# A four-layer graph kernel: late slabs, their sign tests and two weight loads moved within layer 0

## The chip, the cores and the metric

The kernel runs on one core of one Trainium2 chip. The metric is the device time of one execution in microseconds.

## The reference, cut to what matters

x is 2708 x 512, adj is 2708 x 2708, non-negative, with a full diagonal and few other entries. Four layers follow one another, each with a layer norm in front and a residual:

```
h = relu(layernorm(x));  x = x + layer0(h, adj)   # (adj + head) @ h / row sum; head = (adj > 0) / sqrt(count of adj > 0)
h = relu(layernorm(x));  x = x + attention(h, adj)        # scores - 1e16 * (1 - adj), softmax, 8 heads
h = relu(layernorm(x));  x = x + tanh(relu(adj @ (relu(adj @ (h @ W1) + b1) @ W3) + b3) @ Wf + bf)
h = relu(layernorm(x));  x = x + (adj != 0) @ (h @ W + b) / column count
```

With the factor 1e16 the softmax of attention picks one entry of each row, so the kernel only looks for the largest entry of each row of adj (a "search" of the row) and gathers one projected row. It sets flags ("bad") where an input doesn't allow such shortcuts: a negative entry of adj, a tie, weights so large that scores could reach the mask. A general path, in a branch at the end, is taken only then.

## The kernel before

Rows are cut into 22 row tiles of 128 (the last has 20 rows). Layer 0 and the projections of attention are done in one loop over m = 0 to 21, and this loop fills the first third of the time. In turn m:

- PE adds up the products of row tile m into acc (L778), from the incidence blocks that DVE made one turn ahead (`incidence(m + 1)`, lines L617 to L649). These need the norm of the row, spread over the partitions by a product into the PSUM tile rb (L619). The pool of rb has one buffer, and `score_bound` takes the same one for its sum (L466).
- DVE then finishes the row tile: xt (L787), and the statistics of its norm (L172 to L179). ACT applies the norm (hn, L182), PE transposes it (pt, L188), ACT copies it (hT, L189), PE projects it (yacc, L158): that is `after(m - 1)`.
- `stats_to` works ahead on the slabs, the 128 rows of adj that belong to a row tile (1.35 MB, tile name ar, three buffers): signs and counts on ACT (L510, L515), row sums (L529), and the search for the largest entry on DVE (`attended`, L540 to L549: MAX8 and FIND_INDEX8, about 3 us each). The three ar buffers serve the rank lists too (`rank_rows`, `load_ranks` of the last row tile).
- POOL gathers rows of h and blocks of adj by lists (L562, L580), which DVE has made by `search` (L372 to L400) from the ranks.

Row tiles 3, 4, 5, 0, 1, 2 (LATE, in this order) come first in the statistics, and their slabs are dropped there without a search. They are read again in turns m = 15 to 20, one to a turn, for the test for negative entries (`count_signs`: Sign at L497, Relu at L498, compared at L489) and the search. In before, turn 15 asks for the slabs of 3 and 4, and each later turn for the next one.

`score_bound` reads Wq and Wk (1 MB each), squares and sums them on ACT (L464), and makes one flag. `load_w` and `split_w` read W1 (then W3) into one buffer (wr) and split W1 on ACT and DVE (L193 to L203). `behind(dst, last)` is a DVE copy of one element from `last` into `dst` (L425): what writes `dst` afterwards has to wait for it.

A planner of the framework sets the order of the instructions on each engine before the run, the program's order being the priority; it may put a later instruction of the program ahead of an earlier one that isn't ready by its own reckoning. Each engine then works its queue in that order.

Of the kernel before, what the change touches and what calls it, by code (L numbers as in the profile page):

```python
# [42 lines left out]
def kernel(  # L43
# [31 lines left out]
    NT = (N + P - 1) // P  # L75
# [11 lines left out]
    def rows(t):  # L87
        return min(P, N - t * P)

    def dense_of(m):  # L90

        return 0 if m == NT - 1 else DENSE
# [127 lines left out]
    with tc.tile_pool(name="l0_slab", bufs=2) as slabs, tc.tile_pool(  # L220
# [202 lines left out]
        def behind(dst, last):  # L423

            nc.vector.tensor_copy(dst, last)  # L425
# [51 lines left out]
        LATE = FIRST + ZERO  # L477
        masks, row, slab = {}, {}, {}

        def load_slab(m):  # L480
            n = rows(m)
            if m in slab:
                return
            slab[m] = slabs.tile([P, N], FP, name="ar", bufs=3)
            nc.sync.dma_start(out=slab[m][:n], in_=adj[m * P : m * P + n])

        def flag_negative(m, sum_sgn, cnt):
            n = rows(m)
            nc.vector.tensor_tensor(  # L489
                bad[:n, BAD_NEG + m : BAD_NEG + m + 1], sum_sgn[:n], cnt[:n], ALU.not_equal  # L490
            )

        def count_signs(m):

            sgn = slabs.tile([P, N], BF, name="sgn", bufs=GROUP)
            cnt, sum_sgn = (wp.tile([P, 1], FP, name=name, bufs=4) for name in ("cnt", "sum_sgn"))
            nc.scalar.activation(sgn, slab[m], AF.Sign, accum_out=sum_sgn)  # L497
            nc.scalar.activation(sgn, sgn, AF.Relu, accum_out=cnt)  # L498
            flag_negative(m, sum_sgn, cnt)

        def row_norm(m):


            n = rows(m)
            ar = slab[m]

            cnt, sum_sgn = (wp.tile([P, 1], FP, name=name, bufs=4) for name in ("cnt", "sum_sgn"))
            rn, deg = (wp.tile([P, 1], FP, name=name, bufs=10) for name in ("rn", "deg"))
            sgn = slabs.tile([P, N], BF, name="sgn", bufs=GROUP)
            nc.scalar.activation(sgn[:n], ar[:n], AF.Sign, accum_out=sum_sgn[:n])  # L510
            if m in LATE:
                cnt = sum_sgn
                nc.vector.tensor_scalar_max(cnt[:n], cnt[:n], 0.0)
            else:
                nc.scalar.activation(sgn[:n], sgn[:n], AF.Relu, accum_out=cnt[:n])  # L515
            nc.scalar.activation(rn[:n], cnt[:n], AF.Sqrt)
            nc.vector.tensor_scalar_max(rn[:n], rn[:n], NORM_EPS)
            nc.vector.reciprocal(rn[:n], rn[:n])
            if m not in LATE:
                flag_negative(m, sum_sgn, cnt)  # L520
            masks[m], row[m] = sgn, (rn, deg, cnt)
# [13 lines left out]
        def attended(m):  # L535

            n = rows(m)
            cols = slice(m * P, m * P + n)
            ar = slab.pop(m)
            nc.vector.tensor_max(ar[:n, cols], ar[:n, cols], ident[:n, :n])  # L540
            top = wp.tile([P, 8], FP, name="top")
            nc.vector.max(top[:n], ar[:n])
            at_top = wp.tile([P, 8], U32, name="at_top")
            nc.vector.max_index(at_top[:n], top[:n], ar[:n])
            nc.vector.tensor_copy(idx[:n, m : m + 1], at_top[:n, 0:1])
            nc.vector.tensor_scalar(
                top[:n, 0:2], top[:n, 0:2], 1.0, MASK_SCALE, op0=ALU.subtract, op1=ALU.mult
            )
            nc.vector.tensor_tensor(  # L549
                bad[:n, m : m + 1], top[:n, 1:2], top[:n, 0:1], ALU.is_ge  # L550
            )
# [104 lines left out]


        order_n = ZERO[:1] + FIRST + ZERO[1:] + list(range(LEAD + GROUP, NT))
        late = list(LATE)
        normed, near, far = [0], [LEAD], [LEAD]  # L660
        listable = set()

# [3 lines left out]
        def do_next(num=1):  # L666
            for job in todo[:num]:
                if job.func is search and job.args[0] not in ranks_of:
                    load_ranks(job.args[0])
                job()  # L670
                if job.func is search:
                    listable.add(job.args[0])
            del todo[:num]
            if todo and todo[0].func is search and todo[0].args[0] not in ranks_of:
                load_ranks(todo[0].args[0])

        def stats_to(m):


            while normed[0] <= order_n.index(m):  # L680
                t = order_n[normed[0]]
                do_next()
                load_slab(t)
                if normed[0] + 1 < NT:
                    load_slab(order_n[normed[0] + 1])
                row_norm(t)
                row_sum(t)
                if t == 0 or t % GROUP == GROUP - 1 or t >= NT - 2:
                    last_block = count(masks)
                    if t not in ZERO:  # L690
                        if dense_of(t):
                            rank_blocks(list(masks), last_block)
                        else:
                            flush_counts()
                            todo.append(partial(rank_rows, list(masks)))
                        todo.extend(partial(search, k) for k in masks)
                        do_next(0)
                    masks.clear()
                if t in late:
                    slab.pop(t)  # L700
                else:
                    attended(t)
                normed[0] += 1
# [32 lines left out]
        def flush_counts():  # L736
            for issue in pending_c:
                issue()
            pending_c.clear()
# [26 lines left out]
        for m in range(NT):  # L766
            n = rows(m)
            if m + 1 < NT:
                load_x(m + 1)
            if m + 2 < NT and m + 2 >= LEAD and dense_of(m + 2):  # L770
                blocks[m + 2] = load_block(m + 2, tiles_d)
            flush()
            if LEAD <= m + 1 < NT:
                incs[m + 1] = incidence(m + 1)
            acc = ps_acc.tile([P, D], FP, name="acc")
            pairs = incs.pop(m)
            for i, (a, g) in enumerate(pairs):
                nc.tensor.matmul(  # L778
                    acc[:n], a, g, start=(i == 0), stop=(i == len(pairs) - 1)
                )  # L780
            if m + 1 < LEAD:
                stats_to(m + 1)
                incs[m + 1] = incidence(m + 1)
            if m:
                after(m - 1, hns.pop(m - 1))
            xt = xs.pop(m)
            nc.vector.scalar_tensor_tensor(  # L787
                xt[:n], acc[:n], row.pop(m)[1][:n], xt[:n], op0=ALU.mult, op1=ALU.add
            )
            hns[m] = wp.tile([P, D], FP, name="hn")  # L790
            norm(wp, xt, n, hns[m])
            store(m, xt)
            if normed[0] == NT:
                do_next(2 if NT - 8 < m < NT - 5 else 1)
            stats_to(min(2 * m + 6, m + 8, NT - 1))
            gathers_to(m + 2)
            if m + 8 > NT and late:
                if late[0] not in slab:
                    load_slab(late[0])
                if len(late) > 1:  # L800
                    load_slab(late[1])
                count_signs(late[0])
                attended(late.pop(0))
            if m + 8 == NT + 1:
                todo.append(partial(rank_rows, list(range(1, LEAD))))
                todo.extend(partial(search, k) for k in range(1, LEAD))
            if m == NT // 2 + 4:
                score_bound(xt[:1, :1])
            if m == NT - LEAD - 1:
                for t in range(1, LEAD):  # L810
                    gather_adj(t)
            if m == NT // 2 + 6:
                wr = load_w(wset, w1_d, "wr", lambda w: behind(w[:1, 0, :1], xt[:1, :1]))
                w1 = split_w(wset, wr, "wa")
                wr = load_w(wset, w3_d, "wr")
# [430 lines left out]
    for m in order_2:  # L1246
# [16 lines left out]
        if m == NFULL:  # L1263
            xt = wp.tile([P, D], FP, name="u")
        else:

            place = {order_2[-1]: "gs0", NSLOT: f"slot{order_2[-1]}"}.get(m, f"slot{m}")
            xt = x3[m] = gp.tile([P, D], FP, name=place)
# [55 lines left out]
    with tc.If(general > 0):  # L1324

        with tc.tile_pool(name="l0_g", bufs=2) as gp, tc.tile_pool(
# [3 lines left out]
            for t in range(NT):  # L1330
                n = rows(t)
                xt = gp.tile([P, D], FP, name="xt")
# [4 lines left out]
            for m in range(NT):  # L1337
# [35 lines left out]
                xt = gp.tile([P, D], FP, name="xt")  # L1373
# [7 lines left out]
        with tc.tile_pool(name="l1_qkv", bufs=1) as qkvp:  # L1381
# [6 lines left out]
            with tc.tile_pool(name="l1_pw", bufs=1) as pwp, tc.tile_pool(  # L1388
# [13 lines left out]
                for b in range(NB):  # L1402
# [4 lines left out]
                    for t in tiles:  # L1407
                        n = rows(t)
                        o = t * P - c0
                        xt = pxp.tile([P, D], FP, name="xt")  # L1410
# [116 lines left out]
        with ExitStack() as gen:  # L1527
# [94 lines left out]
            for t in range(NT):  # L1622
                n = rows(t)
                xt = wp.tile([P, D], FP, name="xt")
# [19 lines left out]
            for block in range(NB):  # L1644
# [4 lines left out]
                for t in node_tiles(c0, nb):  # L1649
                    n = rows(t)  # L1650
                    xt = wp.tile([P, D], FP, name="xt")
# [98 lines left out]
```

## Time and profile before

| | us |
|---|---|
| median of 3 runs (1505.83 to 1511.4) | 1506.5 |
| profiled execution, its own time | 1444.13 |
| its span | 1442.3 |
| xt (L787) of row tiles 12, 13, 14, 15, 16, 17 | 315.64, 335.21, 350.59, 365.05, 382.69, 406.40 |
| xt of row tiles 18, 19, 20, 21 | 420.46, 443.52, 452.99, 460.94 |
| busy: PE, DVE, ACT, POOL | 1294.6, 942.6, 692.4, 670.7 |

Times in a profile count from the start of the span. A row of the timeline has the start, the duration, the engine with the line of the kernel, the operation, the tile written and the tiles read, and in brackets how long the engine was idle before it and what it waited for. "SPq" and "POOLq" are issues of transfers.

### The profile page before, as it was taken

To read this page: it belongs to the slowest core of one execution; us is meant where nothing else is said; L and a number is where in the kernel's file an instruction comes from. 1 tells how busy PE (TensorE), PEld (TensorE's weight loads), DVE (VectorE), ACT (ScalarE), POOL (GpSimd) and SP (SyncE) were. 2 spreads that over 40 slices of the span, in tenths; PEclk is the share of its full clock that TensorE was granted. 3 is DMA by queue.
4 is the path that set the end of the run, shared out by engine and by line. 5 is a ranking of instruction groups with operands and counts; after the bars stand their busy time and mean duration, and the time that the engine had idled before them with its cause. 6 is when DMAs were issued, how large, how long until landed. Compare 5 with 4: busy or idle time off the path is not lost. (4 is left out here: it accounts for less than half of the span.)

```text
span 1442.3 us, 15447 instructions
## 1 busy us (share of the span) xinstructions
PE 1294.6 (90%) x4400; PEld 767.3 (53%) x4400; DVE 942.6 (65%) x1916; ACT 692.4 (48%) x1054; POOL 670.7 (47%) x690
## 2 busy tenths in 40 slices
PE   3889888999788499899999998999999999688997
PEld 1334333444333366556656664666677666466664
DVE  5597988999898687533434454665666666465574
ACT  8776636542562465323333342445444554354443
POOL 2154667777545320364444432333433445067762
PEclk9999999999899799999999999999999999788998
DMA  9999899998974884587777768555565657378884
GB/s 361 343 307 320 260 340 321 333 283 271 364 291 142 292 276 164 184 274 244 231 221 247 235 223 286 170 180 161 182 186 165 212 180 220 117 238 260 255 260 146
DMA packets 196188, 351.46 MB, mean 244 GB/s; under 512 B 26482, under 2 KB 107940, under 8 KB 192361
## 3 DMA queue, kind: packets, MB, share of 16 engines
q1 hardware_dynamic: 148701, 200.87, 41.3%
q0 software_dynamic: 47392, 149.51, 32.8%
q8 instruction: 37, 0.61, 0.2%
q14 instruction: 58, 0.48, 0.1%
HBM read 287.00 MB, written 63.29 MB: 243 GB/s over the span
## 5 line engine op out<-in xcount | busy, mean ns | idle before, releaser
L987 PE MATMUL aggs<-gg,ac 128*128 128x512 f32 (+1 forms) x520 | 232.3, 594 | 3.5 <-DMA gg<-g1d,idx_g 3.5
L935 POOL DMA_INDIRECT gg<-g2d,idx_g x130 | 131.0, 1008 | 217.7 <-PE aggs L987 169.4
L935 POOL DMA_INDIRECT gg<-g1d,idx_g x130 | 132.5, 1019 | 173.7 <-PE aggs L987 104.1
L562 POOL DMA_INDIRECT ac<-in_adj_t_dram,idx_a x130 | 133.6, 1027 | 96.3 <-issue 33.8
L778 PE MATMUL acc<-h,inc 128*128 128x512 f32 (+1 forms) x348 | 165.0, 616 | 7.1 <-DVE inc L630 7.0
L987 PEld LDWEIGHTS aggs<-gg,ac 128*128 128x128 f32 (+1 forms) x520 | 97.5, 189 | 110.3 <-issue 101.7
L580 POOL DMA_INDIRECT h<-h0d,idx_g x111 | 110.1, 992 | 50.7 <-issue 22.9
L971 ACT ACTIVATE a_hi<-raw 128x384 fp32r<-128x384 f32 x84 | 43.6, 520 | 160.2 <-issue 88.4
L984 PE MATMUL agg<-ghi,a_hi 128*128 128x512 f32 x252 | 114.8, 455 | 4.7 <-ACT a_hi L971 2.5
L778 PEld LDWEIGHTS acc<-h,inc 128*128 128x128 f32 (+1 forms) x348 | 65.4, 197 | 83.0 <-issue 70.9
L984 PE MATMUL agg<-glo,a_lo 128*128 128x512 f32 x252 | 101.9, 404 | 0.0
L158 PE MATMUL yacc<-wvo,hT 128*128 128x512 f32 (+1 forms) x176 | 88.9, 650 | 14.4 <-ACT hT L189 14.4
L778 PE MATMUL acc<-h,incl 128*128 128x512 f32 (+1 forms) x222 | 100.7, 600 | 0.0
L984 PE MATMUL aggs<-gs,a_s 128*128 128x512 f32 x252 | 100.1, 400 | 0.6 <-DVE gs L200 0.6
L935 POOL DMA_INDIRECT gg<-hidr,idx_h x79 | 80.1, 1013 | 44.1 <-issue 13.1
L972 DVE TENSOR_TENSOR a_lo<-raw,a_hi 128x384 fp32r<-128x384 f32 x84 | 47.2, 562 | 76.7 <-ACT a_hi L971 53.9
L881 DVE SCALAR_TENSOR_TENSOR v_lo<-pt,v_hi 128x512 fp32r<-128x512 f32 (+1 forms) x88 | 56.7, 665 | 45.9 <-ACT v_hi L880 45.6
L862 DVE SCALAR_TENSOR_TENSOR u<-aggs,u 128x512 f32<-128x512 f32 x42 | 28.9, 687 | 76.4 <-PE aggs L987 74.8
L510 ACT ACTIVATE sgn<-ar 128x2708 bf16<-128x2708 f32 (+1 forms) x22 | 54.0, 2455 | 35.2 <-DMA ar<-in_adj_dram 35.2
L880 ACT ACTIVATE v_hi<-pt 128x512 fp32r<-128x512 f32 (+1 forms) x88 | 48.8, 578 | 44.2 <-PE pt L875 42.3
L778 PEld LDWEIGHTS acc<-h,incl 128*128 128x128 f32 (+1 forms) x222 | 42.0, 191 | 52.5 <-issue 45.6
L158 PEld LDWEIGHTS yacc<-wvo,hT 128*128 128x128 f32 (+1 forms) x176 | 34.2, 202 | 60.9 <-issue 38.2
(285 smaller groups left out, 2822.2 us busy)
## 6 DMA issues: line engine op xcount, KB each, us to landing
ar<-in_adj_dram SPq DMA_DIRECT2D x27, 1354.0 KB
raw<-in_adj_t_dram SPq DMA_DIRECT2D x108, 192.0 KB
slot<-x SPq DMA_DIRECT2D x41, 256.0 KB
at<-in_adj_t_dram SPq DMA_DIRECT2D x27, 384.0 KB
ranks<-rank_b SPq DMA_DIRECT2D x20, 485.0 KB
ac<-lst SPq DMA_DIRECT2D x16, 384.0 KB
h<-in_x_dram SPq DMA_DIRECT2D x21, 256.0 KB
h0d<-h POOLq DMA_DIRECT2D x21, 256.0 KB, 5.7
```

The lines of the kernel that those rows point to most:

```text
L158: nc.tensor.matmul(acc[:n], hT[:, c, :n], w[:, c, :], start=(c == 0), stop=(c == NCD - 1))
L510: nc.scalar.activation(sgn[:n], ar[:n], AF.Sign, accum_out=sum_sgn[:n])
L562: nc.gpsimd.indirect_dma_start(out=ac[:, c, :n], out_offset=None, in_=adj_units, in_offset=bass.IndirectOffsetOnAxis(ap=idx_a[:, m, c0 + c ...
L580: nc.gpsimd.indirect_dma_start(out=g, out_offset=None, in_=h0d[:, :], in_offset=bass.IndirectOffsetOnAxis(ap=idx_g[:, m, c : c + 1], axis=0),)
L778: nc.tensor.matmul(acc[:n], a, g, start=(i == 0), stop=(i == len(pairs) - 1))
L880: nc.scalar.activation(hi[d], pt[d], AF.Relu, scale=UP)
L881: nc.vector.scalar_tensor_tensor(lo[d], pt[d], 0.0, hi[d].bitcast(FP), op0=ALU.max, op1=ALU.subtract)
L935: nc.gpsimd.indirect_dma_start(out=gs[c], out_offset=None, in_=gd[:, :], in_offset=bass.IndirectOffsetOnAxis(ap=index[:, m, c : c + 1], ax ...
L971: nc.scalar.activation(hi[d], raw, AF.Copy, scale=UP)
L972: nc.vector.tensor_tensor(lo[d], raw, hi[d].bitcast(FP), ALU.subtract)
L984: nc.tensor.matmul(acc[:n], a[:k, i, :n], b[:k], start=st, stop=sp)
L987: nc.tensor.matmul(mixed[:n], a, g, start=(c == 0 and not dense_of(m)), stop=(c == len(chunks) - 1),)
```

## The change

The six late slabs are asked for by turn (`step`): the first in turn 14, the others in turns 15 to 19; the tests and searches stay in turns 15 to 20. Each sign test gets a `behind`, so it can't begin before xt of its turn. `score_bound` moves from turn 15 to turn 12, and the read and split of W1 with the read of W3 from turn 17 to turn 14.

```
-        def count_signs(m):
+        def count_signs(m, last):
             sgn = slabs.tile([P, N], BF, name="sgn", bufs=GROUP)
...
+            behind(sgn[:1, :1], last)
             nc.scalar.activation(sgn, slab[m], AF.Sign, accum_out=sum_sgn)
...
-        late = list(LATE)
...
-                if t in late:
+                if t in LATE:
                     slab.pop(t)
...
-            if m + 8 > NT and late:
-                if late[0] not in slab:
-                    load_slab(late[0])
-                if len(late) > 1:
-                    load_slab(late[1])
-                count_signs(late[0])
-                attended(late.pop(0))
+
+            step = m - (NT - 8)
+            if 0 <= step < len(LATE):
+                load_slab(LATE[step])
+            if 0 < step <= len(LATE):
+                count_signs(LATE[step - 1], xt[:1, :1])
+                attended(LATE[step - 1])
...
-            if m == NT // 2 + 4:
+            if m == NT // 2 + 1:
                 score_bound(xt[:1, :1])
...
-            if m == NT // 2 + 6:
+            if m == NT // 2 + 3:
                 wr = load_w(wset, w1_d, "wr", lambda w: behind(w[:1, 0, :1], xt[:1, :1]))
                 w1 = split_w(wset, wr, "wa")
                 wr = load_w(wset, w3_d, "wr")
```

## The prediction

> **What bounds it now.** The chain of what ended last covers only the last 16 us, so I read the table of stages first, cut at the row tiles of layer 0 (m = 12 to 21), then each engine in order of time. The columns are stage, length, busy us of PE, PE weight loads, DVE, ACT and POOL, clock, DMA share, GB/s.
> ```profile
> 318.00:335.00 17.00, 17.00 (x60) 7.53 (x59) 17.00 (x33) 10.74 (x14) 11.39 (x12) 1.00 0.80 251
> 335.00:350.00 15.00, 14.46 (x41) 6.67 (x40) 14.34 (x34) 2.29 (x4) 10.14 (x11) 1.00 0.87 297
> 350.00:364.00 14.00, 14.00 (x37) 6.30 (x36) 14.00 (x23) 2.18 (x4) 11.77 (x8) 1.00 0.83 253
> 364.00:375.00 11.00, 11.00 (x27) 4.81 (x26) 7.02 (x21) 2.78 (x4) 8.49 (x9) 1.00 0.95 336
> 375.00:390.00 15.00, 6.74 (x15) 3.10 (x14) 13.58 (x16) 13.44 (x15) 8.70 (x10) 0.66 1.02 412
> 390.00:405.00 15.00, 13.01 (x32) 6.00 (x32) 14.42 (x25) 11.57 (x11) 3.89 (x3) 0.89 0.81 296
> 405.00:420.00 15.00, 13.33 (x35) 5.80 (x32) 14.07 (x30) 2.83 (x4) 10.52 (x12) 1.00 1.02 384
> 420.00:440.00 20.00, 16.92 (x46) 7.59 (x47) 17.58 (x36) 15.84 (x22) 7.25 (x8) 1.00 0.65 226
> 440.00:461.00 21.00, 17.63 (x44) 6.82 (x42) 20.63 (x38) 3.25 (x7) 9.20 (x11) 1.00 0.42 130
> ```
> DVE is full from 318 to 364 and nearly full after. Its idle time from 364 to 461 is 3.98 + 1.42 + 0.58 + 0.93 + 2.42 + 0.37 = 9.7 us. That is the size of the prize: DVE's work stays the same, and layer 0 cannot end before it is done. PE has the visible hole, 8.3 us in 375 to 390. PE in order of time:
> ```profile
> 375.45 0.60 PE L188 MATMUL pt<-ident,hn 128*128 128x128 f32 x4
> 384.32 5.44 PE L158 MATMUL yacc<-wvo,hT 128*128 128x512 f32 x6 [8.26 <-ACT hT L189]
> 389.59 0.28 PE L466 MATMUL rb<-sq,ones 128*128 128x2 f32 x2
> ...
> 390.67 0.38 PE L619 MATMUL rb<-dg,ones 128*128 128x128 f32 x2
> ...
> 393.81 6.68 PE L778 MATMUL acc<-h,inc 128*128 128x512 f32 x12
> ```
> Row tile 16 ends at 375.45, row tile 17 starts at 393.81. Between them PE waits for ACT, and the product for tile 17's norm row (rb, L619) comes only after that of the score bound (L466): both use the pool's one rb buffer, and the score bound is earlier in the program (m = 15; tile 17's comes in m = 16). ACT and DVE over the same time:
> ```profile
> 373.80 2.46 ACT L497 ACTIVATE sgn<-ar 128x2708 bf16<-128x2708 f32 x1 [4.90 <-DMA ar<-in_adj_dram]
> ...
> 381.78 1.91 ACT L464 ACTIVATE wa<-wa 128x2048 f32<-128x2048 f32 x1 [0.40 <-DMA wa<-in_L_gnn_Wqs_dram]
> ...
> 383.69 0.58 ACT L189 ACTIVATE hT<-pt 128x512 f32<-128x512 f32 x1
> ...
> 376.38 0.29 DVE L540 TENSOR_TENSOR ar<-ar,ident 128x128 f32<-128x128 f32 x1 [3.45 <-ACT sgn L497]
> ...
> 382.69 0.73 DVE L787 SCALAR_TENSOR_TENSOR xt<-acc,deg,xt 128x512 f32<-128x512 f32 x1
> ```
> ACT runs sign tests and a square that waited for their transfers, with hT queued behind them for 7.6 us. DVE waits 3.45 us for the sign test of slab 3, then its search (6.3 us) stands ahead of xt of tile 16 (L787), whose accumulator was ready at 375.45. SP issued that slab at 363.47, with slab 4, and Wq and Wk at 366.64: 4.8 MB at once (DMA share 1.02).
>
> **What the Trainium skill says.** "Perfetto Trace Analysis", Per-engine timelines: ACT and DVE are strict FIFO. The trace agrees: hT and xt sit behind waiting instructions. "DMA: Bandwidth & Descriptors", Queues, rings and completion order: each DMA engine serves the queues with work in turn, packet by packet; so an added transfer slows the row gathers rather than queueing behind them. The trace only fits this: in 375 to 390 the gathers on POOL pause for landings of earlier ones (1.78, 0.97, 1.30 us).
>
> **The change, part by part.**
> *First late slab one tile sooner.* Slab 3 moves from m = 15 to m = 14; the other five were already asked for one tile ahead, and stay. In the program it is now ahead of the two ar buffers that the ranks of tile 21 take, behind which it was issued (L362 at 363.10, then L485 at 363.47). Its buffer is free once slab 19 (searched by 313), or 20 (327) at the latest, is done. It lands well before tile 15's turn (365). DVE's 3.45 us wait goes. One SP issue (0.33 us) moves; what it moves past on SP are short issues that wait for DVE, no cost. Slab 4 still waits for the ranks' first buffer, about 363.5, as before; slab 5 takes slab 3's buffer some 7 us sooner.
> *Sign test behind its tile.* Six 1x1 DVE copies at 0.14 us (row L425) = 0.84 us on the bounding engine. ACT can no longer take a sign test before xt of its turn, so the pairs at 373.8 and 378.8 (5.1 us each with both passes) stop holding hT of the tile before. Added wait: ACT behind DVE; behind it on ACT are rstd and hn of the same tile, which need xt anyway. It also keeps a late search from standing ahead of xt of its turn (as at 403.51, ahead of 406.40).
> *Score bound, m = 15 to m = 12.* Two 1 MB transfers, two squares (1.9 us), two tiny products, a copy and five DVE operations of 0.14 us move whole, so the sum of work stays. The rb hold moves too: from between tiles 16 and 17 to between 13 and 14. Here it is worth a time. xt of tile 12 is at 315.64; in before the gate (L425) came 1.4 us later and the issues 0.2 and 0.6 us behind it, so Wq and Wk are asked for at about 317.3. 5.4 MB (ranks, two slabs, Wq, Wk) took from 363.1 to the last square's start at 386.6 at the latest, 0.23 MB/us; 2 MB then takes 8 to 9 us, and 3.4 MB, if slab 3 is in the same rush, up to 15. They land at 326 to 332; the last square ends 2 us later, and from there to L619 it was 2.3 us (388.4 to 390.67). So the norm row of tile 14 comes at 330 to 336. In before it was used by DVE at 327.07 and by PE at 332.76. DVE, 17.00 of 17 busy, would stand for 3 to 9 us, unless its order has other work there (the search of slab 20 ends at 327, that of slab 21 is 3.0 + 3.0 us and needs ACT's three passes of 2.46 us, which the squares delay). I take 3.5 us, with 0 and 9 as ends. PE has 3.4 us of projection (333.7 to 337.2) to put ahead, so it loses less.
> *w1, m = 17 to m = 14, and w3.* 1 MB each, and the split: on ACT 4.4 us, on DVE 8 operations of 0.65 = 5.2 us (429.1 to 434.0). Moved, not added. At 352 to 366 DVE is full, so xt of tile 15 slips by up to 5 us; two acc buffers let tile 16 run on, and its end (375.45) leaves time for hn. In return DVE is 5.2 us lighter at 429, and the wait there (1.82 us for L193) may go. Cover: tile 16's 24 products; without it, 5 us earlier and 5 us less later, still nothing net. w3 is not needed before 475.
>
> **The sum**, against the profiled execution (1444.13 us, span 1442.3): DVE idle saved is 3.45 certain plus half of the other 6.2 = 6.5; added 0.84 and 3.5. Net -2.2 us, 1441.9. After 461 the same tail follows, and the stages from 480 on start that much sooner. The runs shown have a median of 1506.5, 62 us above the profiled one; nothing in the change touches that gap, so I carry the difference over: 1504.3.
>
> **Cases.**
> *Trade (0.40):* as summed, 1500 to 1508.
> *All of it (0.22):* Wq and Wk land by 325, DVE keeps working through m = 13, and 9 of the 9.7 us go, 0.8 comes back: 1498.3, to 1495 with the freer PE. For it: DMA is at 0.80 in 318 to 335. Against: the rush with slab 3, and a DVE that can't get below its own work.
> *The hold moved (0.23, slower):* one mechanism, the rb buffer held by the score bound through m = 13. In before it took 25.6 us from xt (365.05) to the next norm row (390.67). The same 25.6 from 315.64 gives 341.2; DVE, standing since 327, loses 14, less 6.5, plus 0.8: +8.3, 1514.8. It decides from a norm row at 332.7 (5.7 us after 327) on; over 340 it is slower by over 0.5%. For it: one buffer, DVE full, ACT's passes for row 21 in the same 321 to 329. Against: half the bytes ahead and no waiting sign tests in front.
> *Not as said (0.15):* five of six slabs are read when they were, and the plan sets the other orders as before: 1506.5 within 2.
>
> **The numbers.** 0.5% is 7.5 us, about what a measurement of this kernel can tell from no change. Faster by more: most of the second case, 0.18. Slower by more: most of the third, 0.21. Same: 0.61. The range runs from the second case's end, 1495, to just past the third's, 1516.
>
> **What would show it.** Slab 3's issue before 345 and no DVE wait for L497 near 376; PE's gap before yacc at 384 (8.26) under 2 us; L466 ahead of 335, and the wait of DVE on L619 or of PE on inc right after it: its length decides. xt of the last tile at 457 to 460 instead of 460.94. The forecast is wrong if that comes before 453 (then DVE was not the bound), or if L619 of tile 14 is after 340.

## The result, and the profile after

| | before | after |
|---|---|---|
| median, us | 1506.5 (19 runs, 1495.66 to 1516.62) | 1510.79 (19 runs, 1498.19 to 1518.94) |
| ratio after / before | | 1.0032, interval 1.0009 to 1.0056 |
| profiled execution, its span | 1444.13, 1442.3 | 1509.41, 1507.6 |

The change makes the kernel slower by 0.3%. That is less than the half per cent that the forecast counted as a change, but the interval leaves out 1.

The two profiled executions can't be set against each other directly. In both, the instructions of every engine come in the same order up to about row tile 12, and yet xt of row tile 12 is at 315.64 us in one and at 355.50 in the other. The experiments show the same two values on different chips (312.7 to 320.1 in e1 to e4, 351.7 to 358.9 in e5 to e8), so the two traces very probably come from different chips. The 62 us that the forecast carried over, between the profiled execution of before and its median, are then a difference of chips too (e1 has a median of 1442.75 us). Times are therefore given here from xt of row tile 12 on, and where sizes matter, copies of both kernels that ran on one chip are compared (e1 and e2).

The table of stages of after, cut at xt of row tiles 12, 13, 14 and 15; the one from row tile 16 to 17; and, last, from xt of row tile 20 to the first gather of rows of y (columns: stage, length, busy us of PE, PE weight loads, DVE, ACT, POOL, clock, DMA share, GB/s):
```profile
355.50:375.12 19.62, 17.20 (x66) 7.49 (x64) 13.99 (x39) 12.91 (x17) 13.62 (x15) 1.00 0.99 336
375.12:396.38 21.26, 18.75 (x40) 8.53 (x41) 17.93 (x38) 4.94 (x9) 6.38 (x7) 0.76 0.81 259
396.38:415.79 19.41, 16.79 (x47) 7.78 (x46) 19.35 (x31) 6.69 (x12) 17.03 (x8) 1.00 0.72 234
...
430.14:453.12 22.98, 17.84 (x41) 7.84 (x40) 19.87 (x34) 7.66 (x9) 18.41 (x16) 0.85 0.80 255
...
497.95:525.89 27.94, 14.42 (x54) 5.65 (x52) 14.62 (x49) 12.32 (x19) 9.31 (x11) 0.81 0.46 138
```
The hole has moved. In before DVE was full over the stage behind row tile 12; here it is busy 13.99 of 19.62 us, and 17.93 of 21.26 in the next. The last line is a stage that the forecast took as unchanged.

ACT in order of time, behind xt of row tile 12 (355.50):
```profile
365.39 2.46 ACT L516 ACTIVATE sgn<-sgn 20x2708 bf16<-20x2708 bf16 x1
...
370.20 1.91 ACT L464 ACTIVATE wa<-wa 128x2048 f32<-128x2048 f32 x1 [2.22 <-DMA wa<-in_L_gnn_Wqs_dram]
...
372.11 0.18 ACT L517 ACTIVATE rn<-cnt 20x1 f32<-20x1 f32 x1
372.20 2.44 ACT L530 ACTIVATE ar<-ar 20x2708 f32<-20x2708 f32 x1
...
374.99 1.91 ACT L464 ACTIVATE wa<-wa 128x2048 f32<-128x2048 f32 x1 [0.25 <-DVE deg L531]
```
The square for Wq (L464) waited 2.22 us for its transfer. Behind it in ACT's queue stand the root (L517) and the row sum (L530) of slab 21, both there for the taking. DVE over the same time:
```profile
372.33 0.14 DVE L518 TENSOR_SCALAR rn<-rn 20x1 f32<-20x1 f32 x1 [2.65 <-issue]
...
374.77 0.21 DVE L531 SCALAR_TENSOR_TENSOR deg<-cnt,rn,rsum 20x1 f32<-20x1 f32 x1 [2.12 <-issue]
...
375.12 0.75 DVE L787 SCALAR_TENSOR_TENSOR xt<-acc,deg,xt 128x512 f32<-128x512 f32 x1
...
380.17 0.16 DVE L468 TENSOR_TENSOR sq<-sq 128x1 f32<-128x1 f32 x1 [1.42 <-ACT sq L467]
```
DVE stands for 2.65, 2.12 and 1.42 us; the releaser is given as "issue", but the instructions after the gaps take rn, the row sum and sq, whose ACT instructions end at the same moments (372.11 + 0.18, 372.20 + 2.44 and its read of 0.18, 379.98 + 0.16). The xt of row tile 13 (L787) is behind the first two. PE:
```profile
377.05 0.59 PE L466 MATMUL rb<-sq,ones 128*128 128x2 f32 x2 [4.34 <-issue]
...
380.19 0.79 PE L620 MATMUL rb<-dg,ones 128*128 128x128 f32 x2 [0.59 <-ACT sq L467]
```
PE waits 4.34 us for the second square, and the norm row of row tile 14 (L620) comes at 380.19, 24.7 us after xt of row tile 12. The forecast's rival had 25.6.

The end of the loop, after:
```profile
497.95 0.73 DVE L787 SCALAR_TENSOR_TENSOR xt<-acc,deg,xt 128x512 f32<-128x512 f32 x1
...
499.39 0.14 DVE L425 CAST sgn<-xt 1x1 bf16<-1x1 f32 x1
...
499.56 2.46 ACT L498 ACTIVATE sgn<-ar 128x2708 bf16<-128x2708 f32 x1 [2.36 <-DVE top L547]
...
502.47 2.98 DVE L543 MAX8 top<-ar 128x8 f32<-128x2708 f32 x1
...
505.57 2.97 DVE L545 FIND_INDEX8 at_top<-top,ar 128x8 uint32<-128x2708 f32 x1
...
508.46 0.20 DVE L179 TENSOR_SCALAR shift<-mv,rstd 128x1 f32<-128x1 f32 x1
...
509.56 1.11 PE L188 MATMUL pt<-ident,hn 128*128 128x128 f32 x4 [8.60 <-ACT hn L182]
```
And before:
```profile
452.99 0.75 DVE L787 SCALAR_TENSOR_TENSOR xt<-acc,deg,xt 128x512 f32<-128x512 f32 x1 [0.37 <-PE acc L778]
...
454.71 2.98 DVE L542 MAX8 top<-ar 128x8 f32<-128x2708 f32 x1
...
457.80 2.97 DVE L544 FIND_INDEX8 at_top<-top,ar 128x8 uint32<-128x2708 f32 x1
...
460.69 0.19 DVE L179 TENSOR_SCALAR shift<-mv,rstd 128x1 f32<-128x1 f32 x1
...
461.79 1.12 PE L188 MATMUL pt<-ident,hn 128*128 128x128 f32 x4 [2.84 <-ACT hn L182]
```
In before the sign test of the last late slab (Sign at 424.81) was long done when its turn came. MAX8 started 1.72 us after xt of row tile 20 (454.71 - 452.99), the shift of row tile 20 followed FIND at 460.69, and PE waited 2.84 us for hn. In after the gate (the one-element copy of `behind`, L425) holds Sign until 499.56, MAX8 starts 4.52 us after xt, the shift comes at 508.46, and PE waits 8.60 us. The shift is 10.51 us behind xt in place of 7.70.

### The profile page after: what moved, and what is told of

Read it like the earlier page. It is cut to its first block, busy times and chain, and to the rows that moved or that the text cites. A ratio compares the mean times of both kernels' runs of the same rounds, so it can differ in the third digit from the quotient of the medians.

```text
span 1507.6 us, 15462 instructions
## 1 busy us (share of the span) xinstructions
PE 1310.1 (87%) x4400; PEld 772.3 (51%) x4400; DVE 944.0 (63%) x1922; ACT 692.3 (46%) x1054; POOL 678.8 (45%) x690
## 4 chain that ended last, share of the span: by engine, by line
PE 59%; DVE 12%; DMA 10%; issue 8%; ACT 6%; another core or an unknown queue 4%; POOL 1%; SPq 0%; POOLq 0%; ACTq 0%; DVEq 0%
PE aggs L987 14%; PE main L900 9%; PE agg L984 7%; PE acc L778 6%; PE mixed L900 4%; PE aggs L984 4%; PE yacc L158 3%; PE agg L1171 3%; PE pt L875 2%; PE aggs L1171 2%; DVE at_top L545 2%; DMA raw<-in_adj_t_dram 2%; DMA ar<-in_adj_dram 2%; DVE top L543 1%
## 5 line engine op out<-in xcount | busy, mean ns | idle before, releaser
L581 POOL DMA_INDIRECT h<-h0d,idx_g x111 | 119.1, 1073 | 57.4 <-issue 28.0
L158 PE MATMUL yacc<-wvo,hT 128*128 128x512 f32 (+1 forms) x176 | 95.0, 689 | 33.4 <-ACT hT L189 32.2
L881 DVE SCALAR_TENSOR_TENSOR v_lo<-pt,v_hi 128x512 fp32r<-128x512 f32 (+1 forms) x88 | 56.6, 664 | 46.8 <-ACT v_hi L880 27.9
L862 DVE SCALAR_TENSOR_TENSOR u<-aggs,u 128x512 f32<-128x512 f32 x42 | 28.8, 687 | 77.9 <-PE aggs L987 76.3
```

Of the source, the lines that this page charges most:

```text
L158: nc.tensor.matmul(acc[:n], hT[:, c, :n], w[:, c, :], start=(c == 0), stop=(c == NCD - 1))
L581: nc.gpsimd.indirect_dma_start(out=g, out_offset=None, in_=h0d[:, :], in_offset=bass.IndirectOffsetOnAxis(ap=idx_g[:, m, c : c + 1], axis=0),)
L881: nc.vector.scalar_tensor_tensor(lo[d], pt[d], 0.0, hi[d].bitcast(FP), op0=ALU.max, op1=ALU.subtract)
```

## The experiments

Ratios are against runs of the kernel before on the same chip, taken together with them. Three chips served: e1 to e4 and e9 to e12 ran on one (before: 1442.32 and 1442.68 us), e5 to e8 on a second (1517.35), e13 to e18 on a third (1442.79 and 1443.56). Two stretches are read from each trace: **loop**, from xt of row tile 12 to xt of row tile 20, with DVE's idle time in it; and **tail**, from there to the first gather from y. Executions of one kernel on one chip scatter by 15 to 21 us (before, with e9 to e12: 1432.4 to 1451.23), and a trace is one of them, so the traces say where and the ratios say how much.

| run | ratio (interval) | loop | DVE idle in it | tail |
|---|---|---|---|---|
| e1 before | 0.9995 (0.9977 to 1.0013) | 137.4 | 10.4 | 24.8 |
| e12, e16 before | | 139.2, 138.4 | 12.3, 11.2 | 25.5, 25.6 |
| e2 after | 1.0049 (1.0033 to 1.0066) | 137.7 | 11.7 | 28.1 |
| e3 after, own bank | 1.0054 (1.0037 to 1.0072) | 138.1 | 12.2 | 34.3 |
| e4 slabs and gates alone | 1.0038 (1.0021 to 1.0056) | 142.7 | 16.1 | 27.6 |
| e5 after, no gates | 1.0040 (1.0014 to 1.0067) | 152.2 | 22.8 | 24.1 |
| e6 gates alone | 0.9990 (0.9964 to 1.0015) | 145.1 | 20.8 | 26.0 |
| e7 weights alone | 1.0034 (1.0009 to 1.0059) | 146.7 | 17.1 | 25.5 |
| e8 before, last step at the end | 0.9991 (0.9971 to 1.0011) | 143.1 | 15.9 | 27.0 |
| e9 before, last search at the end | 0.9983 (0.9967 to 0.9999) | 136.3 | 8.5 | 19.4 |
| e10 after, last search at the end | 1.0010 (0.9989 to 1.0031) | 142.7 | 16.5 | 22.1 |
| e11 after, last gate off | 1.0007 (0.9990 to 1.0023) | 139.8 | 13.7 | 24.6 |
| e13 score bound alone | 1.0078 (1.0055 to 1.0101) | 144.7 | 18.6 | 32.5 |
| e14 slabs alone, last gate off | 1.0010 (0.9989 to 1.0030) | 140.0 | 13.3 | 29.0 |
| e15 weights alone, own bank | 1.0026 (1.0003 to 1.0049) | 150.6 | 21.7 | 26.9 |
| e17 last gate off, score bound in 13 | 0.9994 (0.9976 to 1.0011) | 132.7 | 6.3 | 28.8 |
| e18 after, score bound in 13 | 1.0004 (0.9987 to 1.0020) | 131.5 | 5.2 | 27.4 |

**e1 and e2: both kernels, unchanged, on one chip.**

> The kernel before, unchanged, for a second trace of it. Until xt of row tile 12 both kernels issue the same instructions in the same order, yet that point is at 315.64 us in the trace of before and at 355.50 in that of after. If the first trace was of an unusually quick execution (theory), the span here is near 1500 and xt of tile 12 near 350. If the change had slowed the start (rival), xt of tile 12 stays near 316. From xt of tile 12 to the degrees (L298) the first trace has 157.2 us, after 162.0; theory: 157 +- 3 here too.

> The changed kernel again: ratio 1.003, and 162 +- 3 us from xt of tile 12 to the degrees, with the norm row of tile 14 (L620) 24 to 26 us behind xt of tile 12. If that stretch is only chance (rival), it scatters by more than the 4.8 us between the two kernels.

DVE's waits in the loop, before (e1; columns: what waited and for what, us in total, times, longest):
```profile
DVE ar L540 <- ACT sgn L497: 4.3, 1, 4.3
DVE end L372 <- DMA ar<-rank_l: 1.6, 1, 1.6
...
DVE wa L195 <- ACT wa L193: 1.3, 1, 1.3
```
After (e2):
```profile
DVE rn L518 <- ACT rn L517: 5.0, 1, 5.0
DVE deg L531 <- ACT ar L530: 2.1, 1, 2.1
DVE incl L623 <- PE rb L620: 1.1, 1, 1.1
...
DVE ar L541 <- ACT sgn L498: 0.7, 1, 0.7
```
The wait for slab 3's sign test went (4.3 to 0.7). In its place are 5.0 us for the root of slab 21 and 2.1 for its row sum. DVE was busy 126.94 us of the loop in e1 and 126.07 in e2, idle 10.4 and 11.7: the loop is as long as it was, and what the change costs here in the trace is in the tail, 24.8 to 28.1 us. That is some 3.7 us for both stretches, where the ratio of this chip stands for 7; the traces don't show the rest.

On the start, e1's theory and its rival both failed: xt of row tile 12 is at 312.7 in e1 and at 313.0 in e2, so neither was the first trace unusually quick, nor does the change slow the start. The stretch to the degrees is 156.3 us in e1, as expected, and 157.7 in e2, short of the 162 +- 3 that were expected; the norm row of row tile 14 came at 24.9 us, as expected.

**e3: the score bound's sum out of rb.** All of the change, but the sum goes into a buffer of another pool:

```
-            tot = ps_small.tile([P, P], FP, name="rb")
+            tot = ps_list.tile([P, BLK], FP, name="list")
```

> The changed kernel, but the sum of the score bound goes to a PSUM tile of the list pool (three buffers) in place of the one rb buffer. Theory (the rb hold moved to tile 14 costs 6 us there): the norm row of tile 14 comes within 8 us of xt of tile 12, tile 13 to 14 shrinks from 21.3 to about 15.5 us, the stretch from tile 12 to the degrees is 155 to 157 us, ratio 0.998 to 1.000. Rival (DVE's total work sets the end, w1's split comes in front of xt of tile 15): the norm row comes early, but the stretch stays at 160 to 163, ratio 1.003.

1.0054, no better than the change, so the theory failed: a free rb alone brings no time. But the trace shows what rb does in front of row tile 13. In before DVE had the incidence of row tile 14 to make (L622, L630) while ACT passed over slab 21; its norm row came 5.3 us behind xt of row tile 12 (e1):
```profile
324.12 0.94 DVE L622 SCALAR_TENSOR_TENSOR inc<-at,rb 128x768 f32<-128x768 f32 x1
...
328.02 0.13 DVE L517 TENSOR_SCALAR rn<-rn 20x1 f32<-20x1 f32 x1
```
In e2 that norm row stands behind the score bound and comes at 24.9 us. The incidence comes after the root, and DVE stands:
```profile
331.17 0.14 DVE L518 TENSOR_SCALAR rn<-rn 20x1 f32<-20x1 f32 x1 [5.01 <-ACT rn L517]
...
338.54 0.96 DVE L623 SCALAR_TENSOR_TENSOR inc<-at,rb 128x768 f32<-128x768 f32 x1 [0.24 <-PE rb L620]
```
In e3 the square still stands ahead of the root and waits 3.84 us for Wq, but the norm row comes at 11.7 us, and the incidence fills most of the time:
```profile
332.87 0.94 DVE L623 SCALAR_TENSOR_TENSOR inc<-at,rb 128x768 f32<-128x768 f32 x1
...
337.11 0.14 DVE L518 TENSOR_SCALAR rn<-rn 20x1 f32<-20x1 f32 x1 [0.64 <-ACT rn L517]
```
By these traces the 5.0 us of e2 take two things: the square in front of the root, and the held rb, which keeps from DVE the work that it had there. What e3 wins comes back elsewhere: DVE waits 5.1 us for W1's first halves (L193), and the tail grows to 34.3.

**e4 and e7: the two halves of the change.** e4 is the change with the score bound back in turn 15 and W1 in 17; e7 is the kernel before with the score bound in turn 12 and W1 in 14:

```
-            if m == NT // 2 + 4:
+            if m == NT // 2 + 1:
                 score_bound(xt[:1, :1])
...
-            if m == NT // 2 + 6:
+            if m == NT // 2 + 3:
```

> Only the slabs and their sign tests of the change; the score bound and W1 back in turns 15 and 17. Theory: the hold is back between tiles 16 and 17, the wait for slab 3 is gone; stretch 153 to 157 us, ratio 0.997 to 1.000. Rival (the gate of the sign tests is what costs, by pushing the last search behind xt of tile 21): the last search comes after xt of tile 21 here too, and the stretch is 160 or more, ratio 1.002 to 1.005.

> The kernel before with the score bound in turn 12 and W1 in turn 14; slabs and sign tests as in before. Theory (DVE's work from tile 12 to 20 is 127 us of 137 whatever the order, so a moved stall is worth nothing): stretch from xt of tile 12 to 20 stays at 137 +- 2 us, ratio 0.998 to 1.002. Rival (the rb hold at tile 14 and the split ahead of xt of tile 15 are lost time): stretch 141 or more, ratio 1.003 and over.

Each half costs by itself what the whole does: 1.0038 and 1.0034 against 1.0032 and 1.0049. The costs don't add up. Both miss what the theory expected and lie where the rivals put them: the gates (e4), the hold and the split (e7). There is no trace of before from e7's chip, so its stretches have nothing to stand against.

**e5 and e6: no gates, and gates alone.** e5 is the change without `behind(sgn[:1, :1], last)`; e6 adds that line to the kernel before, with xt of the turn as `last`.

> The changed kernel without the gate of the sign tests; slabs one turn ahead and weights sooner stay. Theory (the gate puts the sign test of the last slab in series: xt of tile 20, the copy, 2.5 us of sign test, then the 6 us search, with hn of tiles 20 and 21 behind it): the sign test of the last slab is over before xt of tile 20, the last search (FIND_INDEX8) starts 4.5 to 5 us behind xt of tile 20 as in before (7.7 in the changed kernel), and the ratio goes from 1.005 to 1.001 to 1.003. Rival (the moved weights cost): ratio stays at 1.004 to 1.006.

> The kernel before with the gate of the sign tests alone; slabs, score bound and W1 as in before. Theory: last search 7 to 8 us behind xt of tile 20, ratio 1.002 to 1.004. Rival (the gate is covered, the slab's earlier read is what costs): last search under 5 us behind xt of tile 20, ratio within 0.001 of 1.

Without gates the change still costs 0.4%, though its tail is short (24.1 us), as the theory said; its loop is long. The gates by themselves cost nothing that shows, against the theory. e6's order fits the second:
```profile
499.09 0.74 DVE L789 SCALAR_TENSOR_TENSOR xt<-acc,deg,xt 128x512 f32<-128x512 f32 x1
...
504.44 2.45 ACT L499 ACTIVATE sgn<-ar 128x2708 bf16<-128x2708 f32 x1
...
505.25 0.18 DVE L179 TENSOR_SCALAR shift<-mv,rstd 128x1 f32<-128x1 f32 x1
...
507.34 2.98 DVE L544 MAX8 top<-ar 128x8 f32<-128x2708 f32 x1
```
Here the plan put the shift of row tile 20 ahead of MAX8 of the last search, 6.16 us after xt, so that the sign test delays hn of row tile 20 by some 1.4 us (506.88, behind Sign on ACT) and the search delays nothing. So a gate's price here is not that of its copy alone; it depends on what the plan puts behind the gated instruction.

**e8: the last late step at the end.** The kernel before, with the whole step of the last late slab in turn 21, its Sign gated on hn of row tile 21:

```
-            if m + 8 > NT and late:
+            if m + 8 > NT and late and (len(late) > 1 or m == NT - 1):
...
-                count_signs(late[0])
+                count_signs(late[0], hns[m][:1, :1] if m == NT - 1 else None)
```

> The kernel before with one step moved: the test and search of the last late slab (row tile 2) go from turn 20 to turn 21 and wait for hn of tile 21, so that hn of tiles 20 and 21, and the projections behind them, come ahead of the search on DVE. Theory (the tail is a chain: last search on DVE, hn of tile 20 and 21, projection, y, first gather of y, 25 us from xt of tile 20 to the gather): xt of tile 21 within 3 us of xt of tile 20, PE's wait between the last projections under 3 us, first gather of y 3 to 6 us sooner, ratio 0.996 to 0.998. Rival (the pool's memory comes free only after the search, so the next stage waits for it instead): ratio 0.999 to 1.003.

0.9991, no change, as the rival had it, for another reason. The search left the path, but its second pass on ACT (Relu) now stood ahead of the last hT, and PE waited 4.14 us for that.

**e9, e10, e11: the tail.** e11 is the change with the gate left off one sign test:

```
-            behind(sgn[:1, :1], last)
+            if m != LATE[-1]:
+                behind(sgn[:1, :1], last)
```

e9 is the kernel before with the last search alone held back (its sign test stays early), e10 the same on e11:

```
+            if last is not None:
+                behind(top[:1, :1], last)
             nc.vector.max(top[:n], ar[:n])
...
+                elif m == NT - 1:
+                    attended(late.pop(0), hns[m][:1, :1])
```

> The changed kernel with the gate left off the sign test of the last late slab alone, so that ACT may run it before xt of row tile 20. Theory 'tail': MAX8 of the last search starts right behind the statistics of row tile 20, 2.6 us sooner; the stretch from xt of row tile 20 to the first gather from y falls from 28 to 25.5 us, the ratio from 1.003-1.005 to 1.001-1.003. Rival 'loop': 1.003 to 1.005 as before.

> The changed kernel with the sign test of the last late slab ungated, and the search of that slab behind hn of the last row tile, as in e9. Theory 'tail': the net loss of the change comes from the last slab's sign test (2.6 us) in front of the last search, and the search itself (6 us) stands on the path; without both the ratio is 0.997 to 1.000. Rival 'loop': the loss lies in row tiles 13 to 20, in the orders that the plan sets there, and the ratio stays at 1.002 or more even with a shorter tail.

> The kernel before with one change: the search of the last late slab (row tile 2) waits, by a one-element copy ahead of its MAX8, for hn of the last row tile; its sign test stays early. Theory 'tail': in the kernel before the 6 us of that search stand on DVE ahead of the shift of row tile 20, so they lie on the path to the last rows of y and the first gather from y (24.8 to 25.4 us after xt of row tile 20). With the search behind, this stretch falls to 19 to 22 us and the ratio is 0.996 to 0.998. Rival: the path there is set by POOL's own list gathers or by PE, and the ratio is 0.999 to 1.001.

> The kernel before unchanged, for a trace on the same chip as e9 to e11. Both theories: xt of row tile 20 at 137 us after that of row tile 12, the first gather from y 25 us later.

e11 falls from 1.0049 to 1.0007 on the same chip, and the two intervals don't meet. Its tail:
```profile
449.20 2.45 ACT L499 ACTIVATE sgn<-ar 128x2708 bf16<-128x2708 f32 x1
...
455.51 2.96 DVE L544 MAX8 top<-ar 128x8 f32<-128x2708 f32 x1
...
459.05 0.18 DVE L179 TENSOR_SCALAR shift<-mv,rstd 128x1 f32<-128x1 f32 x1
...
459.24 2.96 DVE L546 FIND_INDEX8 at_top<-top,ar 128x8 uint32<-128x2708 f32 x1
```
The last Sign starts at 449.20, ahead of xt of row tile 20 (453.07). MAX8 starts 2.44 us after xt, the shift comes between MAX8 and FIND at 5.98, and the tail is 24.6 us. hn of that row tile starts at 461.30, 8.2 us behind xt, where it was 10.7 in after. So in this order one of the six gates makes up most of what the change costs. It is no fixed price: e5 leaves off this gate with the other five and stays at 1.0040, on another chip and with a loop of 152.2 us. Nor do the stretches add up to the ratio here, since the tail is 3.5 us shorter than in e2 and the loop 2.1 longer.

e9 shows the search in front of the shift as a cost that the kernel before has already:
```profile
451.72 0.21 DVE L179 TENSOR_SCALAR shift<-mv,rstd 128x1 f32<-128x1 f32 x1
...
457.59 0.20 DVE L179 TENSOR_SCALAR shift<-mv,rstd 20x1 f32<-20x1 f32 x1
...
458.84 2.98 DVE L544 MAX8 top<-ar 128x8 f32<-128x2708 f32 x1
```
Both shifts are done before MAX8 starts. The tail falls to 19.4 us, as expected, the ratio to 0.9983, a little short of what was expected. e10 shortens the tail too (22.1), but its loop is longer by 2.9 us than e11's and the ratio is 1.0010, which meets neither theory.

**e13 and e15: which part of the weights.** e13 is the kernel before with the score bound in turn 12 alone; e15 is e7 with e3's line.

> The kernel before with the score bound in turn 12 alone; W1 and W3 stay in turn 17, the late slabs as before. Theory 'hold': what the weights alone cost (1.0034 in e7) comes from the score bound holding rb while row tile 14 needs it, so the ratio is 1.002 to 1.004. Rival 'split': it comes from the split of W1 on a full DVE ahead of xt of row tile 15, and the score bound alone costs nothing: 0.999 to 1.001.

> The kernel of e7 (score bound in turn 12, W1 and W3 in turn 14, late slabs as before) with the score bound's sum in the PSUM pool of the lists in place of the one rb buffer. Theory 'hold': the ratio falls from 1.0034 to 1.000 to 1.001. Rival 'split' or the order of the plan: 1.002 to 1.004 as in e7.

> The kernel before unchanged, for a trace on the same chip as e13 to e15. Every theory: xt of row tile 20 some 137 to 145 us after that of row tile 12, the first gather from y 25 us later.

The score bound alone is the dearest version of all, 1.0078, about twice what the theory of the hold expected, and the rival had it near 1. In its loop DVE has 126.13 us of work, as ever, and 18.6 idle. So W1 in turn 14 is not what makes the weights dear; leaving it in turn 17 makes nothing better (the intervals of e13 and e7 just touch, on two chips). With a bank of its own (e15) the weights cost 1.0026, which its interval can't tell from e7's 1.0034. That is where the rival had it. So neither e3's nor e15's ratio speaks for the hold as what costs the time; the intervals are too wide to rule out a part of it.

**e14: e4 without the last gate.**

> The kernel of e4 (late slabs one tile sooner and gated, weights where they were before) with the gate left off the last late slab's sign test. Theory 'tail': e4's 1.0038 came from the last sign test in front of the last search; the stretch from xt of row tile 20 to the first gather from y falls from 27.6 to about 25 us and the ratio to 1.000 to 1.002. Rival 'loop': e4 lost 5 us between row tiles 12 and 20, and the ratio stays at 1.003 or more.

The ratio falls from 1.0038 to 1.0010, as the tail theory said. The place does not fit: the tail is 29.0 us, not 25, and the loop is 2.7 us shorter than e4's. In e4 the shift of row tile 20 (462.85) stands ahead of MAX8 (462.96) in spite of the gate, so what the gate did in after isn't seen there. The intervals overlap as well; the pair is no second proof of the gate's cost.

**e17 and e18: the score bound one turn later.** e18 is the change with the score bound in turn 13, e17 is e11 with the same line.

```
-            if m == NT // 2 + 1:
+            if m == NT // 2 + 2:
                 score_bound(xt[:1, :1])
```

> The changed kernel, all gates on, with the score bound in turn 13 in place of 12. Theory 'square ahead of the root': 3 to 7 us less than the change, ratio 1.000 to 1.002; the stretch from xt of row tile 20 to the first gather from y still about 28 us, since the last sign test keeps its gate. Rivals 'hold' and 'transfers': 1.003 to 1.005 as the change.

> The kernel of e11 (the change, with no gate on the last late slab's sign test) and the score bound in turn 13 in place of 12, so that on ACT its squares stand behind the root and the row sum of slab 21. Theory 'square ahead of the root': in e11 DVE waits 4.8 and 2.1 us for that root and that row sum because the square waits for Wq in front of them; with the squares behind, these 6.9 us go, row tile 20 comes 3 to 7 us sooner than in e11 (139.8 us after row tile 12), and the ratio is 0.996 to 0.999. Rival 'hold': what delays row tiles 14 and 15 is the score bound in rb, which now meets row tile 15; row tile 20 no sooner than in e11, ratio 1.000 to 1.003. Rival 'transfers': Wq and Wk slow the gathers wherever they are; also no gain.

ACT in e18:
```profile
326.74 2.45 ACT L530 ACTIVATE ar<-ar 20x2708 f32<-20x2708 f32 x1
...
329.19 0.18 ACT L517 ACTIVATE rn<-cnt 20x1 f32<-20x1 f32 x1
...
351.90 1.91 ACT L464 ACTIVATE wa<-wa 128x2048 f32<-128x2048 f32 x1 [7.63 <-DMA wa<-in_L_gnn_Wqs_dram]
```
The row sum and the root of slab 21 now stand ahead of the square, which waits for its transfer as before, 7.63 us. It still holds up hT behind it, and PE waits 7.11 us for that (354.43), but DVE has other work meanwhile. The loop of e2 (first) and of e18, by stage table:
```profile
312.98:450.72 137.74, 123.12 (x330) 55.65 (x329) 126.07 (x248) 60.45 (x78) 86.30 (x75) 0.95 0.83 282
```
```profile
315.77:447.29 131.52, 119.47 (x327) 53.57 (x326) 126.34 (x247) 60.19 (x78) 84.05 (x76) 0.97 0.85 295
```
The same DVE work, 126.07 and 126.34 us, in 137.74 and in 131.52. The ratio falls from 1.0049 (or 1.0032) to 1.0004, on another chip than either. So the place of the score bound costs, as the theory said. Which part of it costs is not told apart, because the move takes both away from the root: the squares stand behind it, and rb is free for row tile 14, whose norm row comes at 321.04, 5.3 us behind xt of row tile 12 as in e1. The hold now meets row tile 15, whose xt comes 60.8 us behind that of row tile 12 (58.4 in e2), and the gain shows only later (row tile 18 at 101.7 us, in e2 at 113.6).

The two causes don't add up. Taking either away, the gate (e11) or the place of the score bound (e18), leaves the ratio within 0.1% of 1, and taking both (e17, 0.9994) can't be told from either; e17 is above the 0.996 to 0.999 that were expected of it, though its loop is 7.1 us shorter than e11's.

In e18 the loop is 6.9 us shorter than in before on the same chip (e16), but the time is the same as before's. The trace of e17 shows what is late next:
```profile
467.63 0.59 POOL L573 DMA_DIRECT2D lst<-ac  x1 [3.62 <-DMA ac<-in_adj_t_dram,idx_a]
...
471.10 2.19 ACT L193 ACTIVATE wb<-wr 128x512 fp32r<-128x512 f32 x4 [2.27 <-DMA lst<-ac]
```
POOL's last list goes out at 467.63, having waited 3.62 us for a gather of adjacency rows, and ACT waits for that write until 471.10; 17 us lie between xt of row tile 20 (450.54) and that list, where in e11 it was 12.9. Counted from row tile 12, row tile 20 comes 7.1 us sooner than in e11 (132.7 for 139.8), that list 2.9 (149.8 for 152.7), and the first gather from y 3.0. So by this trace more than half of what the loop wins is lost again before the next stage.

## Why the prediction was wrong

The sum had -2.2 us; the measurement has +4.8 (0.32% of 1506.5). Two terms failed: the tail, taken as unchanged with 0.84 us for all gates, grew by 2.6 us in after and 3.3 in e2; and the score bound, taken at 3.5 us, cost DVE 7.4 in e2. Step by step:

- **What bounds the loop: right, but not all that the sum made of it.** DVE's work between row tiles 12 and 20 is 124 to 130 us in every trace of the table, so the loop's length goes with DVE's idle time. The sum then let the later stages start as much sooner as the loop ends. In e18 the loop is 6.9 us shorter than in e16, and the time is not shorter.
- **Slab 3 sooner: right.** SP issues it at 351.94, ahead of xt of row tile 12, and DVE's wait for its sign test went.
- **"6.5 us saved": about right.** From xt of row tile 15 on, DVE's idle time is 10.3 us in e1 and 4.2 in e2: 6.1 saved. What was saved there came back ahead of row tile 14, as the next point tells.
- **The score bound's 3.5 us: the term of the loop that was mis-sized.** Between xt of row tiles 12 and 14 DVE stands 7.4 us in e2 and 0.1 in e1. The place and the kind of loss were as forecast: the norm row of row tile 14 is late, and slab 21's passes on ACT, the work that might have covered it, are held up by the squares. The forecast's text has both halves; it took 3.5 between the ends of 0 and 9. It expected the norm row at 330 to 336 on the scale of before, and it came at 340.5, since ACT took the root and the row sum of slab 21 between the two squares. In e2, 5.0 of the 7.4 us are a wait for the root behind a square that itself waits for Wq, 2.1 are for the row sum right behind that root, and 0.24 are for the norm row. ACT being a strict queue was in the text, from the Trainium skill ("Perfetto Trace Analysis", Per-engine timelines), and the trace of e2 agrees: the root was free to run from 324.0 and started at 330.95, behind the square. e18, with the score bound one turn later, brings the time back; whether by the squares or by rb is open.
- **The gates' 0.84 us: the step that failed in the tail.** Six copies were counted, and "behind it on ACT are rstd and hn of the same tile, which need xt anyway". What waits for the sign test is also the search on DVE, and behind the last search the plan had put the shift of row tile 20. The gate on the last one put 2.8 us on the path (the shift at 10.51 in place of 7.70). e11 takes that gate off and gets 0.42% back, in its order (e5 does not).
- **"After 461 the same tail follows": wrong** for the same reason; 25.4 to 27.9 us.
- **W1 at "still nothing net": not tried alone.** Its split did stand on DVE right ahead of xt of row tile 15 (410.99 to 415.79 in after), as forecast. With it the score bound costs 1.0034 (e7), without it 1.0078 (e13), which speaks against a loss of its own, though on two chips.
- **The rival "the hold moved"** had the sign and the place: the norm row of row tile 14 at 25.6 us, measured 24.7, and "over 340" is where it lay (315.64 + 24.7 = 340.3), a sign by which the forecast called itself wrong. It had DVE lose 14 us there, and DVE lost 7.4, because it had slab 21 and xt of row tile 13 to work on before the norm row came. Its cause, the rb buffer, has a part in DVE's wait (e3's trace), but freeing rb gained no time in e3 or e15.
- The sign that the last tile would come at 457 to 460 misled. It came 139.3 us behind row tile 12 in e2, 454.9 on the scale of before, because the plan put xt of row tile 21 ahead of the last search, not because DVE had less to do.

Three things stay open. The idle time comes at a different place in each variant (the root of slab 21 in e2, W1's split in e3, the rank rows in e15), and why e13's and e15's plans are so much worse was not taken apart. And loops and tails of single traces don't sum up to the ratios: e15's stretches are 13.5 us longer than e16's, its ratio 0.26%.

The third is the clock. Each execution has a mean granted clock of TensorE on record, and within one kernel on one chip those with 0.01 less took some 11 us more (all experiments pooled; correlation -0.67). It was 0.9573 in before and 0.9545 in e2, so by an estimate from that slope 3 of e2's 7 us go along with it. Of the 3.8 us between e4 and e14 it is 2.6. Between e2 and e11, or e2 and e18, most of the difference is left. Whether the order of a kernel changes the clock, or the clock differs for another reason, was not tested.

Of the versions tried, e9 beats both kernels, by 0.17% (0.01 to 0.33) against before; that is the best of many, its interval barely leaves out 1, and by the same estimate over half of it goes along with the clock (0.9586 for 0.9572).

## What to carry to other kernels

An instruction that waits for a transfer costs what is queued behind it on its engine; when it is moved, look at the new place for what stands behind it and for the work that the waiting engine would have had, not only at the old one for what becomes free. A gate on work that is off the path can still cost, when the consumer of that work stands in a queue ahead of something on the path (after, against e6, where it stood behind); check it for the last iteration by itself. When the bounding engine's work stays the same, compare its idle time over the whole stage, since a planner that sets the order anew can give back elsewhere every wait that is taken away; and then look at what is late next, since a shorter stage alone doesn't make a shorter kernel (e18).

## What the runs showed that was not expected

The same kernel took 1442.3 to 1443.6 us on two chips and 1517.35 on a third, 5% apart, and some 40 of those 75 us lie ahead of row tile 12. The ratios of two kernels were measured on one chip each time, and there are none here that compare chips; a trace from one chip can't be subtracted from a trace from another.
